# A transformer block in fp32: the gated layer's second projection with seven products in place of eight in three of its four blocks

## Chip, cores and metric

The kernel runs on one core of a Trainium2 chip. The metric is the device time of one execution in microseconds (us). The core has five engines with their own instruction queues: TensorE (PE in the profile; its weight loads are listed apart, as PEld), VectorE (DVE), ScalarE (ACT), GpSimd (POOL) and SyncE (SP), which here issues most of the DMAs. An instruction waits at the head of its engine's queue until the semaphores that it names have been reached.

## Reference

One block on `x` of shape (2, 1024, 256) with a context of shape (2, 154, 192), 16 heads of 64, all in fp32:

```python
h = layernorm(x, ln1_g, ln1_b)
x = attention(h, h, sa_wq, sa_wk, sa_wv, sa_wo, sa_bo) + x
h = layernorm(x, ln2_g, ln2_b)
x = attention(h, cond_emb, ca_wq, ca_wk, ca_wv, ca_wo, ca_bo) + x
h = layernorm(x, ln3_g, ln3_b)
p = h @ ff_w1 + ff_b1                      # 256 -> 2 * 1024
a, gate = p[..., :1024], p[..., 1024:]
h = a * gelu(gate) @ ff_w2 + ff_b2         # 1024 -> 256: the second projection
return h + x
```

The change touches the last product, `(a * gelu(gate)) @ ff_w2`, and what is added to it.

## Kernel before

The kernel has three stages: self-attention, cross-attention and the gated layer. The order of all instructions is written by hand (`tc.manual_schedule()`); the lists `later`, `sums`, `side`, `work` hold small pieces that the main loops take from in a fixed number per step. The framework puts in semaphores for the dependences between engines.

**Tokens and blocks.** The 2048 tokens are 16 tiles of 128 tokens; `xt` keeps all of them on chip. The gated layer works on NPR = 4 blocks (the code calls one a `pair`) of 512 tokens, each with two halves `j` of BT = 256 tokens. The 1024 features are NF = 8 chunks `f` of 128.

**First projection.** The loop `for k in range(2 * FU)` (L1309) has 64 steps. Steps 2n and 2n+1 handle unit n, that is feature chunk f = n % 8 of block n // 8. `gate_first(n)` and `gate_second(n)` issue seven calls of `product` (L1021) for each unit, one of them (number 4, in `gate_last`) a step late; each has 128 x 128 weights and 256 moving columns, and is two matmul instructions in the profile, all of line L1029. DVE adds the partial products in PSUM to the tile `own` (L1052, L1054, L1068, L1071, L1080), ACT copies one (L1048) and evaluates the two gelus (L1066, L1072), and POOL multiplies the two results into `ub[block][j][:, f, :]`, the input of the second projection: L1073 for j = 1 in `gate_second`, L1082 for j = 0 in `gate_last`, which `gate_first` of the next unit calls.

**Second projection.** When chunk 7 of a block is through, `gate_last` puts 32 slots into `sums`: 4 token tiles `i` by 8 chunks. `sum_slot` (L1088) is one call of matmul, 128 tokens by 256 outputs, adding up over the 8 chunks in one PSUM bank; after the eighth, DVE adds the bank to `xt` (L1105) and a DMA stores 128 KB to `out`. The loop takes two slots per step, so block 0 is summed in steps 16 to 31, while block 1 goes through the first projection, and so on. Block 3 has no next block: its 32 slots are issued one after another behind the loop (L1334).

**Other work on POOL in these steps.** `token_sums` (L1006) prepares a block's tokens for the seven products, in steps 8, 24 and 40. `add_biases("ff", b)` leaves in `later` one addition of `ff_b2` per token tile (L324); from step 17 on the loop takes one per step:

```python
if later and (k <= len(CG) + 2 or k > 2 * NF):
    later.pop(0)()
```

**Buffers.** `w2` (`ff_w2`, 8 chunks of 256 outputs) lies with `w1` in one of the two buffers of the tag `pT`; the other held the transposed attention weights of the cross stage and is out of use by step 18. The tile `ends` belongs to the cross stage too. `sum_tile` takes turns between two PSUM banks.

Of the kernel before, what the change touches and what calls it, by code (L numbers as in the profile page):

```python
# [8 lines left out]
F32 = mybir.dt.float32  # L9
AF = mybir.ActivationFunctionType  # L10
ALU = mybir.AluOpType
AX = mybir.AxisListType

P = 128
# [4 lines left out]
def tile_transformer_block(ctx: ExitStack, tc: tile.TileContext, a: dict, out: bass.AP):  # L19
    nc = tc.nc  # L20
    x, cond = a["x"], a["ctx_768"]
    w = {k[len("L0_xattn_"):]: v for k, v in a.items() if k.startswith("L0_xattn_")}
# [9 lines left out]
    NT = S // P  # L32
    GT = 4
# [14 lines left out]
    QH = S // 2  # L48
    GH = QH // QG
    NK = HB // KB  # L50
    TG = HB // T
    NF = DF // P
    SH = GH // 2
    TF = 2
# [8 lines left out]
    pt_ = ctx.enter_context(tc.tile_pool(name="pt", bufs=2))  # L63
# [9 lines left out]
    def sum_tile(name):  # L73

        return ps_o.tile([P, HB], F32, tag="po", name=name)


    xt = {
        (b, g): const.tile([P, GT, D], F32, tag=f"x{b}{g}", name=f"x{b}{g}")
        for b in range(B) for g in range(NG)  # L80
    }
# [10 lines left out]
    names = ["ln1_g", "ln1_b", "ln2_g", "ln2_b", "ln3_g", "ln3_b", "ff_b1"]  # L92
# [5 lines left out]
    for n in names:  # L98
        k = n_of[n]
# [8 lines left out]
    for n in names[:2]:  # L108
        for r0 in range(0, P, HR):
            (nc.scalar if n == names[0] else nc.sync).dma_start(  # L110
                out=cols[r0:r0 + HR, row_of[n]:row_of[n] + NH],
                in_=w[n].rearrange("(r p) -> p r", p=HR),
# [54 lines left out]
    for n in names[2:]:  # L167
        own = rows[row_of[n] - n_cols:row_of[n] - n_cols + n_of[n], :]
        p = HR if n in twice else P
# [42 lines left out]
    ends = const.tile([P, DA // 2], F32, tag="ends", name="ends")  # L212
# [159 lines left out]
    def take_both(dst, pq, mul=None, t0=0, n=S // 2, shared=False):  # L372

        for r in range(2):
            k0, own = r * S // 2 + t0, pq[r][:, :n]
            if mul is not None:
                if shared and r:
                    nc.vector.tensor_scalar(
                        dst[:, k0:k0 + n], own, mul, 1.0, op0=ALU.mult, op1=ALU.mult)
                else:  # L380
                    nc.scalar.activation(dst[:, k0:k0 + n], own, AF.Copy, scale=mul)  # L381
                continue

            dk = dst.rearrange("p (h n j) -> p n h j", h=2, j=KB)[:, k0 // QG:(k0 + n) // QG]
            own = own.rearrange("p (n h j) -> p n h j", h=2, j=KB)
            if shared and r:
                nc.vector.tensor_copy(dk, own)
            else:
                nc.scalar.copy(dk, own)
# [94 lines left out]
    def out_order(kind):  # L484

        return [t for t in tile_order("ff" if kind == "ca" else "ca") if t % 2 == 0]
# [73 lines left out]
    later = []  # L560

    def run(piece):
        done = piece()
        if done is not None:
            (adds if getattr(done, "adds", False) else stores).append(done)

    def flush(queue):
        for fn in queue:
            fn()
        queue.clear()  # L570

    def run_work(n, n_side, bank=None, n_sum=0):

        while n > 0 and work:
            n -= work[0].banks
            run(work.pop(0))
        for _ in range(min(n_side, len(side))):  # L580
            needs_bank, needs, fn = side[0]
            if needs_bank and not bank and n <= 0 or not added.issuperset(needs):
                break
            if needs_bank and not bank:
                n -= 1
            spare["bank"] = bank or mm_tile
            run(fn)
            side.pop(0)
        for i in range(min(max(n, 0) + n_sum, len(outs))):
            spare["out"] = mm_tile if i < n else sum_tile  # L590
            run(outs.pop(0))

    def out_pieces(kind, b, half, tiles):
        outs.extend(lambda t=t: out_piece(kind, b, half, t) for t in tiles)
# [136 lines left out]
    CG = [(t, min(TG, NT - t)) for t in range(0, NT, TG)]  # L731
# [205 lines left out]
    def cross_drain(c):  # L937

        n = c - 2
        if 0 <= n < CA:  # L940
            cross_turn(n)

    def cross_weigh(c):

        ui, n = divmod(c - 2 * len(CG) - 1, len(CG))
        if n == 0 and 0 <= ui < NU:
            for part in range(2):
                run(lambda: cross_values(ui, part))
            flush(stores)


    NPR = B * 2
    BT = S // 4
    FU = NPR * NF
    wsum, wh, ub, psum, pools = {}, {}, {}, {}, {}
# [65 lines left out]
    def product(n, i, into, first):  # L1021

        pair, f = divmod(n, NF)
        own = slice(f * P, (f + 1) * P)
        lhs = {
            1: w1[:, 0, 1, own], 2: w1[:, 1, 1, own], 3: wsum[4][:, own], 4: w1[:, 1, 0, own],
            5: wsum[1][:, own], 6: wsum[2][:, own], 7: w1[:, 0, 0, own],
        }[i]
        nc.tensor.matmul(  # L1029
            into[:, :BT], lhsT=lhs, rhs=wh[pair][i], start=first, stop=True,  # L1030
            skip_group_check=True)
# [24 lines left out]
    def biases(n):  # L1056
        c = row_of["ff_b1"] + n % NF
        return cols[:, c:c + 1], cols[:, c + NF:c + NF + 1]
# [16 lines left out]
    def gate_last(n):  # L1075

        pair, f = divmod(n, NF)
        pa, pb, pc, own = psum.pop(n)
        product(n, 4, pb, False)
        nc.vector.scalar_tensor_tensor(  # L1080
            own[:, 0, :], pb[:, :BT], biases(n)[0], own[:, 0, :], op0=ALU.add, op1=ALU.add)
        nc.gpsimd.tensor_tensor(ub[pair][0][:, f, :], own[:, 0, :], own[:, 3, :], ALU.mult)  # L1082
        if f == NF - 1:
            sums.extend((pair, i, e) for i in range(2 * TF) for e in range(NF))

    sums, summed = [], {}

    def sum_slot():  # L1088

        pair, i, f = sums.pop(0)  # L1090
        if f == 0:
            summed[pair] = sum_tile(f"pf{pair}_{i}")
        own = summed[pair]
        j, e = divmod(i, TF)
        nc.tensor.matmul(  # L1095
            own[:, :D], lhsT=ub[pair][j][:, f, e * P:(e + 1) * P], rhs=w2[:, f, :],
            start=(f == 0), stop=(f == NF - 1),
        )
        if f < NF - 1:
            return None  # L1100
        b, t = divmod(pair * 2 * TF + i, NT)

        def store():
            xs = xt[b, t // GT][:, t % GT, :]
            nc.vector.tensor_tensor(xs, own[:, :D], xs, ALU.add)  # L1105
            (nc.scalar if pair == NPR - 1 and i % 2 else nc.sync).dma_start(
                out=out[b, t * P:(t + 1) * P, :], in_=xs)

        return store


    with tc.manual_schedule():
# [11 lines left out]
        own = [ps_s.tile([P, 2, HB], F32, tag="s", name=f"first_{r}") for r in range(2)]  # L1124
# [7 lines left out]
        def take(what, i):  # L1132
            at = banks[what] if i < 2 else banks["k2"]
            take_both(qk["sa", 0, 0]["qk".index(what)], at, scale if what == "q" else None,
                      i * P, 2 * P, shared=True)
# [36 lines left out]
        for p in range(SA):  # L1172
# [18 lines left out]
            h, hg = divmod(p, SH)  # L1191
            ui, n = divmod(p, 2 * SH)
# [8 lines left out]
            if hg == LAG:  # L1201
                f = (ui - NPAIR // 2 - 1) * EC
# [10 lines left out]
        for c in range(CA):  # L1213
# [7 lines left out]
            if c == SH + 1:  # L1221

                w1, w2, parts = hold_gated()
# [3 lines left out]
            ui, n = divmod(c, len(CG))  # L1227
# [53 lines left out]
            elif n == 2:  # L1281
# [3 lines left out]
                elif ui == HP:  # L1285
                    wo["ca"] = const.tile([P, NPAIR, D], F32, tag="wo", name="ca_wo")
                    later[:0] = [lambda i=i: nc.sync.dma_start(
                        out=wo["ca"][:, i, :], in_=w["ca_wo"][i * P:(i + 1) * P, :])
# [20 lines left out]
        for k in range(2 * FU):  # L1309
            c = CA + k  # L1310
            if k == 0:
                run_work(0, 0, n_sum=2)
            flush(adds)
            (gate_second if k % 2 else gate_first)(k // 2)
            flush(stores)
            flush(lates)
            if k == 2 * len(CG) + 1:
                norm_beside("ff", B - 1)
            cross_drain(c)
            if k % 2:  # L1320
                cross_weigh(c - 1 if k == len(CG) + 2 else c)
            cross_regroup(c)
            if k == len(CG) + 2:
                out_pieces("ca", B - 1, NQ - 1, out_order("ca"))
            if k % (2 * NF) == NF and k < 2 * FU - 2 * NF:
                token_sums(k // (2 * NF) + 1)
            for _ in range(min(2, len(sums))):
                run(sum_slot)
            flush(stores)
            run_work(0 if k == 1 else 1 + k % 2, k % 2)  # L1330
            if later and (k <= len(CG) + 2 or k > 2 * NF):
                later.pop(0)()
        gate_last(FU - 1)
        while sums:  # L1334
            run(sum_slot)
            flush(stores)


# [31 lines left out]
```

## Time and profile before

| | |
|---|---|
| median of 3 runs | 1082.71 us (1082.28 to 1084.15) |
| profiled execution, own time | 1084.96 us |
| its span | 1083.2 us |
| granted TensorE clock | 1.00 |
| PE busy | 1067.0 us, 99% of the span |
| DVE / POOL / ACT busy | 878.7 / 727.1 / 643.5 us (81 / 67 / 59%) |
| second projection, L1095 | 256 matmul instructions of 128 x 256, 63.2 us busy |
| first projection, L1029 | 448 matmul instructions of 128 x 256 |

The span is the time from the first to the last instruction of the profiled execution; 1.8 us of that execution's own time lie outside it. Busy times of PE count a matmul from its start to its modelled end, so that two that follow each other overlap in the records: what one costs is seen from the distance of the starts, called the pitch below.

### The profile page before, as it was taken

Reading aid. Unit: us, or ns where it says so; the run is one execution under the profiler, and the core shown is the slowest. Engines: PE = TensorE matmul, PEld = TensorE weight load, DVE = VectorE, ACT = ScalarE, POOL = GpSimd, SP = SyncE. Lnnn points to the kernel's source line nnn. Section 1 sums busy time; section 2 is a strip of 40 time slices with the busy share of each in tenths; the row PEclk is TensorE's granted clock in tenths of the full one; section 3 lists DMA queues with packets and bytes.
Section 4 is the critical chain, followed back from the end, with each engine's and each line's share of the span. In section 5 each row is a group of like instructions: output and inputs, shape, how many; then the busy total and the mean of one; then the engine's idle time right before and its main releaser. Section 6 shows DMA issues by size and latency. Waiting matters only on the chain.

```text
span 1083.2 us, 46388 instructions
## 1 busy us (share of the span) xinstructions
PE 1067.0 (99%) x19156; PEld 703.2 (65%) x19156; DVE 878.7 (81%) x1297; ACT 643.5 (59%) x2062; POOL 727.1 (67%) x1552
## 2 busy tenths in 40 slices
PE   8999999999999999999999999999999999999998
PEld 6556556556565565575665655566776677788887
DVE  5799999998989989999999889968877887654442
ACT  5766666777667657666776776656555554242321
POOL 2677777777777777677777777776756785475321
PEclk9999999999999999999999999999999999999999
DMA  3222122112111121111111101136765545000000
GB/s 91 68 70 52 39 48 53 43 43 50 32 43 34 30 50 38 34 43 34 33 42 25 43 14 38 29 79 150 191 157 125 119 107 118 1 10 15 11 14 30
DMA packets 104724, 60.81 MB, mean 56 GB/s; under 512 B 32378, under 2 KB 95298, under 8 KB 104514
## 3 DMA queue, kind: packets, MB, share of 16 engines
q1 hardware_dynamic: 103138, 57.07, 22.2%
q8 instruction: 151, 2.47, 1.0%
q10 hardware_dynamic: 1376, 0.79, 0.2%
q14 instruction: 59, 0.48, 0.1%
HBM read 27.91 MB, written 2.10 MB: 28 GB/s over the span
## 4 chain that ended last, share of the span: by engine, by line
PE 83%; DVE 4%; POOL 4%; DMA 3%; SPq 2%; ACT 2%; issue 1%; POOLq 0%; DVEq 0%; ACTq 0%
PE po L549 18%; PE s L497 17%; PE py_sa L471 5%; PE pf L1095 5%; PE py_ca L471 5%; PE pk_sa L366 4%; PE pv_sa L397 4%; PE poc L908 4%; PE pq_ca L366 4%; PE pq_sa L366 4%; PE pb L1029 4%; DMA st<-st 3%; PE sc L828 2%; PE pa L1029 2%; PE pc L1029 2%; SPq L518 2%
## 5 line engine op out<-in xcount | busy, mean ns | idle before, releaser
L619 POOL TENSOR_SCALAR p<-p,rd,ee 128x512 f32<-128x512 f32 x512 | 390.4, 768 | 90.8 <-DVE rd L609 87.7
L508 ACT ACTIVATE p<-s,st 128x512 f32<-128x512 f32 x512 | 345.0, 686 | 171.1 <-DVE st L681 163.7
L681 DVE TENSOR_REDUCE st<-s 128x2 f32<-128x1024 f32 x256 | 308.5, 1206 | 56.9 <-issue 19.0
L644 DVE STREAM_TRANSPOSE pT<-p 128x1024 f32<-128x1024 f32 x256 | 302.7, 1219 | 2.4 <-POOL p L619 2.1
L497 PE MATMUL s<-k_sa,q_sa 64*32 64x512 f32 x4096 | 252.8, 591 | 3.3 <-ACT p L508 2.5
L549 PE MATMUL po<-pT,v_sa 64*32 64x256 f32 x8192 | 237.1, 376 | 1.0 <-DVE pT L644 1.0
L549 PEld LDWEIGHTS po<-pT,v_sa 64*32 64x32 f32 x8192 | 172.9, 106 | 76.2 <-issue 31.2
L497 PEld LDWEIGHTS s<-k_sa,q_sa 64*32 64x32 f32 x4096 | 78.4, 106 | 104.6 <-issue 57.6
L845 ACT ACTIVATE p<-sc,neg 128x154 f32<-128x154 f32 x256 | 96.1, 403 | 83.0 <-DVE rden L853 79.3
L856 POOL TENSOR_SCALAR p<-p,rden 128x154 f32<-128x154 f32 x256 | 96.8, 398 | 56.7 <-DVE rden L853 56.5
L508 ACT ACTIVATION_READ_ACCUMULATOR p<-s,st 128x1 f32 x512 | 103.9, 203 | 0.0
L526 POOL TENSOR_TENSOR dd<-st 128x8 f32<-128x8 f32 x128 | 25.6, 200 | 74.9 <-DMA st<-st 73.0
L397 PEld LDWEIGHTS pv_sa<-sa_wv,hT_ln 64*128 64x128 f32 x1024 | 58.5, 188 | 14.2 <-issue 8.4
L397 PE MATMUL pv_sa<-sa_wv,hT_ln 64*128 64x128 f32 x1024 | 61.8, 275 | 0.0
L471 PE MATMUL py_ca<-ca_wo,o_ca 128*128 128x256 f32 x256 | 60.0, 382 | 0.5 <-DVE o_ca L922 0.5
L366 PE MATMUL pq_ca<-hT_ln,ca_wq 64*64 64x512 f32 (+1 forms) x544 | 60.1, 590 | 0.0
L471 PE MATMUL py_sa<-sa_wo,o_sa 128*128 128x256 f32 x256 | 59.7, 385 | 0.2 <-ACT v_sa L406 0.2
L471 PEld LDWEIGHTS py_sa<-sa_wo,o_sa 128*128 128x128 f32 x256 | 47.3, 190 | 18.2 <-issue 6.9
L834 DVE TENSOR_REDUCE neg<-sc 128x6 f32<-128x924 f32 (+1 forms) x48 | 47.9, 998 | 13.7 <-PE sc L828 13.3
L366 PE MATMUL pq_sa<-hT_ln,sa_wq 64*32 64x512 f32 (+1 forms) x976 | 56.6, 586 | 0.0
L366 PE MATMUL pk_sa<-hT_ln,sa_wk 64*32 64x512 f32 x960 | 56.2, 590 | 0.3 <-ACT q_sa L381 0.3
L845 ACT ACTIVATION_READ_ACCUMULATOR p<-sc,neg 128x1 f32 x256 | 56.1, 219 | 0.0
(121 smaller groups left out, 1418.9 us busy)
## 6 DMA issues: line engine op xcount, KB each, us to landing
wf<-pT_ca SPq DMA_DIRECT2D x128, 128.0 KB
st<-st SPq DMA_DIRECT2D x512, 1.0 KB
v_sa<-v_sa SPq DMA_DIRECT2D x32, 256.0 KB
sa_wq<-in_L_xattn_sa_wq_dram SPq DMA_DIRECT2D x32, 128.0 KB
sa_wk<-in_L_xattn_sa_wk_dram SPq DMA_DIRECT2D x32, 128.0 KB
sa_wv<-in_L_xattn_sa_wv_dram SPq DMA_DIRECT2D x32, 128.0 KB
ca_wq<-in_L_xattn_ca_wq_dram SPq DMA_DIRECT2D x32, 128.0 KB
wf<-in_L_xattn_ff_w_dram SPq DMA_DIRECT2D x12, 256.0 KB
```

Of the source, the lines that this page charges most:

```text
L366: nc.tensor.matmul(pq[r][f:f + m, at:at + n], lhsT=wt[own, c, f:f + m], rhs=h[own, c, t0:t0 + n], start=(c == 0), stop=(c == NH - 1), tile ...
L397: nc.tensor.matmul(pv[r][:, i * P:(i + 1) * P], lhsT=h[own, c, i * P:(i + 1) * P], rhs=wt[own, c, :], start=(c == 0), stop=(c == NH - 1), ...
L471: nc.tensor.matmul(py[:, e * D:(e + 1) * D], lhsT=o[:, i, (t + e) * P:(t + e + 1) * P], rhs=wo[kind][:, g * HP + i, :], start=(i == 0), st ...
L497: nc.tensor.matmul(sc[a4 * KB:(a4 + 1) * KB, j, :], lhsT=q[r, c:c + KB], rhs=k[r, h * HB:(h + 1) * HB], start=True, stop=True, tile_positi ...
L508: nc.scalar.activation(pr[:, j, :], sc[:, j, :], AF.Exp, bias=st[:, 0, 0, i, j:j + 1], accum_out=st[:, 0, 1, i, j:j + 1],)
L549: nc.tensor.matmul(po[a2][d:d + KB, :QH // 2], lhsT=v[r, t, e, d:d + KB], rhs=pT[r, d // DH * NK + n, :], start=(t == 0 and e == 0), stop= ...
L619: nc.gpsimd.tensor_scalar(pr[:, j, :], pr[:, j, :], own["rd"][:, c:c + 1], own["ee"][:, 0, c:c + 1], op0=ALU.mult, op1=ALU.mult,)
L644: nc.vector.transpose(halves[h][:, :, c:c + KB], slots[p]["p"][i].rearrange("p j (n k) -> p (j n) k", k=KB))
L681: nc.vector.tensor_reduce(st[:, 0, 0, i, :], sc[i], AX.X, ALU.max, negate=True)
L845: nc.scalar.activation(pr_[:, j, i, :T], sc[:, j, i * T:(i + 1) * T], AF.Exp, bias=neg[:, j, i:i + 1], accum_out=den[:, j, i:i + 1],)
L856: nc.gpsimd.tensor_scalar(pr_[:, j, i, :T], pr_[:, j, i, :T], rden[:, j, i:i + 1], 1.0, op0=ALU.mult, op1=ALU.mult,)
L1029: nc.tensor.matmul(into[:, :BT], lhsT=lhs, rhs=wh[pair][i], start=first, stop=True, skip_group_check=True)
```

## The change

In blocks 1, 2 and 3 (`FAST`) the second projection is no longer 8 chunks added up. The features are split into even and odd chunks, the 256 tokens of a half into two tiles, and the outputs into two halves of 128, so that the product is one of 2 x 2 blocks; seven block products take the place of eight, with sums of the inputs beforehand and sums of the results behind.

- `hold_quick` takes a new tile in the free `pT` buffer for the sums, and two pieces of `ends` for copies.
- `quick_weights` makes four combinations of `w2`, each 128 x 512 elements, on POOL (put in at step 18).
- `quick_tokens` makes four combinations per half and even/odd couple of chunks, each 128 x 128, on POOL; one of them overwrites a quarter of `ub`. The list `combos` holds them; each step takes two. For the last unit, half 1 has its four on DVE.
- `fast_sum` is one of the seven products: four calls of matmul (eight instructions) of 128 tokens by 128 outputs. Products 0 and 1 share a PSUM bank, so do 2 to 4, and 5 and 6, the later added onto the earlier; between two of them the partial sum is read. Behind product 0 ACT copies the bank and POOL (DVE in the last block) adds the copy to three quarters of the two token tiles; behind each other product DVE adds the bank to one quarter. A step takes one `fast_sum`; a block has 14 (two halves by seven). The two stores of a half follow products 5 and 6.
- In the last block the two halves take turns, product by product, with more PSUM banks.
- From step 17 on, a bias addition is taken only in odd steps.

```diff
--- before.py
+++ after.py
@@ -1080,14 +1080,117 @@
         nc.vector.scalar_tensor_tensor(
             own[:, 0, :], pb[:, :BT], biases(n)[0], own[:, 0, :], op0=ALU.add, op1=ALU.add)
         nc.gpsimd.tensor_tensor(ub[pair][0][:, f, :], own[:, 0, :], own[:, 3, :], ALU.mult)
-        if f == NF - 1:
-            sums.extend((pair, i, e) for i in range(2 * TF) for e in range(NF))
-
-    sums, summed = [], {}
-
-    def sum_slot():
-
-        pair, i, f = sums.pop(0)
+        if pair in FAST and f % 2:
+            for j in (1, 0) if pair == NPR - 1 else (0, 1):
+                engine = nc.vector if n == FU - 1 and j else nc.gpsimd
+                combos.extend(((pair, j), fn) for fn in quick_tokens(pair, j, f // 2, engine))
+        if f == NF - 1 and pair in FAST:
+            order = [(j, g) for j in range(2) for g in range(7)]
+            if pair == NPR - 1:
+                order = [(j, g) for g in range(7) for j in (1, 0)]
+            sums.extend((lambda j=j, g=g: fast_sum(pair, j, g), 2) for j, g in order)
+        elif f == NF - 1:
+            sums.extend(
+                (lambda i=i, e=e: sum_slot(pair, i, e), 1) for i in range(2 * TF) for e in range(NF))
+
+    sums, summed, quick, combos, mixed = [], {}, {}, [], {}
+    FAST = range(1, NPR)
+    NHF = NF // 2
+
+    def hold_quick():
+
+        own = pt_.tile([P, 2 * NK, QH // 2], F32, tag="pT", name="quick").rearrange("p a b -> p (a b)")
+        at = 0
+
+        def take(*dims):
+            nonlocal at
+            n = 1
+            for d in dims:
+                n *= d
+            view = own[:, at:at + n]
+            at += n
+            names = "abc"[:len(dims)]
+            return view.rearrange(
+                f"p ({' '.join(names)}) -> p {' '.join(names)}", **dict(zip(names, dims)))
+
+        for i in (1, 2, 3, 4):
+            quick["w", i] = take(NHF, P)
+        for i in range(4):
+            quick["u", i] = take(3, NHF, P)
+        for i in range(2):
+            quick["own", i] = ends[:, i * P:(i + 1) * P]
+
+    def quick_weights():
+
+        (b11, b12), (b21, b22) = (
+            [w2[:, h::2, d * P:(d + 1) * P] for d in range(2)] for h in range(2))
+        t1, t2, t3, t4 = (quick["w", i] for i in (1, 2, 3, 4))
+        tt = nc.gpsimd.tensor_tensor
+        return [
+            lambda: tt(t1, b12, b11, ALU.subtract),
+            lambda: tt(t2, b22, t1, ALU.subtract),
+            lambda: tt(t3, b22, b12, ALU.subtract),
+            lambda: tt(t4, b21, t2, ALU.subtract),
+        ]
+
+    def quick_tokens(pair, j, c, engine=nc.gpsimd):
+
+        u, own = ub[pair][j], quick["u", (2 * pair + j) % 4]
+        (a11, a12), (a21, a22) = (
+            [u[:, 2 * c + h, e * P:(e + 1) * P] for h in range(2)] for e in range(2))
+        s1, s2, s4 = (own[:, i, c, :] for i in range(3))
+        tt = engine.tensor_tensor
+        mixed[pair, j] = mixed.get((pair, j), 0) + 1
+        return [
+            lambda: tt(s1, a21, a22, ALU.add),
+            lambda: tt(s2, s1, a11, ALU.subtract),
+            lambda: tt(a21, a11, a21, ALU.subtract),
+            lambda: tt(s4, a12, s2, ALU.subtract),
+        ]
+
+    def fast_sum(pair, j, g):
+
+        u, own = ub[pair][j], quick["u", (2 * pair + j) % 4]
+        (a11, a12), (a21, a22) = (
+            [u[:, h::2, e * P:(e + 1) * P] for h in range(2)] for e in range(2))
+        assert g < 2 or mixed[pair, j] == NHF and (pair, j) not in [key for key, _ in combos]
+        lhs = (a11, a12, own[:, 1], a21, a22, own[:, 0], own[:, 2])[g]
+        rhs = (
+            w2[:, ::2, :P], w2[:, 1::2, :P], quick["w", 2], quick["w", 3], quick["w", 4],
+            quick["w", 1], w2[:, 1::2, P:])[g]
+        if g in (0, 2, 5):
+            bank = sum_tile
+            if pair == NPR - 1:
+                bank = {0: sum_tile, 2: mm_tile, 5: part_tile}[g]
+            summed[j] = bank(f"pq{pair}_{j}_{g}")
+        into = summed[j][:, :P]
+        for c in range(NHF):
+            nc.tensor.matmul(
+                into, lhsT=lhs[:, c, :], rhs=rhs[:, c, :], start=(g in (0, 2, 5) and c == 0),
+                stop=(c == NHF - 1), skip_group_check=True)
+        b, t = divmod(pair * 2 * TF + 2 * j, NT)
+        xs = xt[b, t // GT][:, t % GT:t % GT + 2, :].rearrange("p t (h d) -> p (t h) d", d=P)
+
+        def store():
+            if g == 0:
+                nc.scalar.copy(quick["own", j], into)
+                (nc.vector if pair == NPR - 1 else nc.gpsimd).tensor_tensor(
+                    xs[:, 1:, :], xs[:, 1:, :],
+                    quick["own", j].unsqueeze(1).to_broadcast([P, 3, P]), ALU.add)
+                return
+            q = (None, 0, 1, 3, 2, 3, 1)[g]
+            nc.vector.tensor_tensor(xs[:, q, :], into, xs[:, q, :], ALU.add)
+            if g > 4:
+                e = 6 - g
+                queue = nc.scalar if pair == NPR - 1 and e else nc.sync
+                queue.dma_start(
+                    out=out[b, (t + e) * P:(t + e + 1) * P, :],
+                    in_=xt[b, (t + e) // GT][:, (t + e) % GT, :])
+
+        return store
+
+    def sum_slot(pair, i, f):
+
         if f == 0:
             summed[pair] = sum_tile(f"pf{pair}_{i}")
         own = summed[pair]
@@ -1324,15 +1427,26 @@
                 out_pieces("ca", B - 1, NQ - 1, out_order("ca"))
             if k % (2 * NF) == NF and k < 2 * FU - 2 * NF:
                 token_sums(k // (2 * NF) + 1)
-            for _ in range(min(2, len(sums))):
-                run(sum_slot)
+            n_left = 2
+            while n_left > 0 and sums:
+                fn, n = sums.pop(0)
+                n_left -= n
+                run(fn)
             flush(stores)
+            if k == 2 * NF + 2:
+                hold_quick()
+                combos[:0] = [(None, fn) for fn in quick_weights()]
+            for _ in range(min(2, len(combos))):
+                combos.pop(0)[1]()
             run_work(0 if k == 1 else 1 + k % 2, k % 2)
             if later and (k <= len(CG) + 2 or k > 2 * NF):
-                later.pop(0)()
+                if k <= len(CG) + 2 or k % 2:
+                    later.pop(0)()
         gate_last(FU - 1)
+        while combos:
+            combos.pop(0)[1]()
         while sums:
-            run(sum_slot)
+            run(sums.pop(0)[0])
             flush(stores)
```

## Prediction

> **What bounds the kernel now.** I read the page first, then a table of windows over the last 128 us, where the edited code runs, then the waits there, and last the timeline around single instructions.
>
> ```profile
> span 1083.2 us, 46388 instructions
> PE 1067.0 (99%) x19156; PEld 703.2 (65%) x19156; DVE 878.7 (81%) x1297; ACT 643.5 (59%) x2062; POOL 727.1 (67%) x1552
> PEclk9999999999999999999999999999999999999999
> ```
>
> TensorE (PE) is busy from end to end at the full clock. The windows are cut at the steps in which block 0, 1 and 2 are summed (16 to 31, 32 to 47, 48 to 63), and the tail with block 3:
>
> ```profile
> core 0: us, PE busy (x) PEld busy (x) DVE busy (x) ACT busy (x) POOL busy (x), PEclk, DMA share, GB/s
> 955.00:991.00 36.00, 36.00 (x173) 31.69 (x172) 17.20 (x42) 12.20 (x27) 24.47 (x36) 1.00 0.04 12
> 991.00:1028.00 37.00, 37.00 (x173) 32.58 (x172) 18.16 (x44) 10.46 (x23) 14.01 (x21) 1.00 0.04 15
> 1028.00:1066.00 38.00, 38.00 (x178) 33.45 (x177) 18.74 (x45) 10.83 (x24) 11.63 (x17) 1.00 0.05 15
> 1066.00:1083.20 17.20, 13.85 (x65) 11.85 (x63) 2.25 (x6) 0.00 (x0) 1.28 (x2) 1.00 0.11 38
> ```
>
> PE has no idle time until the tail ends; VectorE (DVE) is half free; GpSimd (POOL) is two thirds full in the first window and a third in the next two. The waits between 960 and 1081 us say the same: POOL, ACT and DVE wait for PE or for each other, and no row names PE as the one that waits. So here the time is what PE issues. The rows that carry the summing:
>
> ```profile
> DVE x L1105 <- PE pf L1095: 17.5, 16, 3.0
> 1065.88 13.98 PE L1095 MATMUL pf<-wf,u 128*128 128x256 f32 x64
> 1079.89 0.42 DVE L1105 TENSOR_TENSOR x<-pf,x 128x256 f32<-128x256 f32 x1 [3.03 <-PE pf L1095]
> ```
>
> The tail's 64 instructions start (13.98 - 0.38) / 63 = 0.2158 us apart (0.38 is the modelled length of the last). That is the pitch of every 128x256 matmul in the stage.
>
> **Part 1: the products.** Removed for each of three blocks: 32 calls, 64 instructions of 256 columns, 64 x 0.2158 = 13.81 us. Added: 14 products of 8 instructions with 128 columns, 112 in all. Seven for eight saves only if half the columns take half the time, although each instruction still loads 128x128 weights, with a recorded length of 190 ns. The trace has 128-column matmuls on the whole array, the transposes, and an fp32 projection directly behind them:
>
> ```profile
> 960.54 0.60 PE L284 MATMUL ph_ln<-ident,xn_ln 128*128 128x128 f32 x4
> 960.98 0.60 PE L1029 MATMUL pa<-hT_ln,wf 128*128 128x256 f32 x2
> 960.87 0.19 PEld L1029 LDWEIGHTS pa<-hT_ln,wf 128*128 128x128 f32 x1
> ...
> 9.40 1.16 PE L366 MATMUL first<-hT_ln,sa_wq 64*128 64x128 f32 x16
> ```
>
> Four 128-column instructions and then the projection: (960.98 - 960.54) / 4 = 0.11, more exactly (0.60 - 0.273) / 3 = 0.109 us apart, 0.273 being the median length of one. The last of these four gaps holds the very load in question: the projection's 190 ns load starts at 960.87, with the last transpose, and its matmul 0.11 us later. So the end of a load's record lies beside the start of its own matmul. 112 x 0.1093 = 12.24 us, a gain of 1.57 us a block, 4.71 us in three. The less kind row: the first stage's query projection, sixteen 64x128 instructions in pairs (last line), takes (1.16 - 0.272) / 15 = 0.059 for one, 0.118 for a pair; 112 x 0.118 = 13.22, a gain of 0.59 a block, 1.8 in all. I take 0.1093, from the same tile shape and stage, and keep 1.8 for the range.
>
> A rule speaks against this. The Trainium skill, page "TensorE: Matmul & The Clock Gate", section "The mechanism" of the part on packing small matmuls, says that a weight load runs beside matmuls in flight only when the row groups differ, and here all instructions use all rows. Taken at its word, the record's 190 ns would stand ahead of each 109 ns matmul, 112 x 0.299 = 33.5 us, or 59 us slower in three blocks, an estimate by that page. The rows above show a load inside the preceding matmul of the same rows, so the row decides.
>
> **Part 2: reading a bank between two products.** Within a group of a half (0-1, 2-3-4, 5-6) the next product adds to a bank that must be read first: four waits a half. What PE waits for: the last instruction's record ends 0.16 us after PE is free for the next (0.273 - 0.109); 0.04 until DVE starts; the addition, 128 columns, is 0.30 us by the line through 256 columns (425 ns) and 512 (653); about 0.05 back. That is 0.55 us; the ACT copy of product 0 is shorter (L777, 128x128: 259 ns). One product a step leaves six instructions (`gate_second`, 1.30 us) or eight (`gate_first`, 1.73 us) between them, and DVE's own additions of that step are through by then (in the trace the last ends 0.25 us before the old slots do). In the tail the other half's product, 0.87 us, lies between. Cost nothing; without that cover, 16 waits in blocks 1 and 2 would cost up to 8.8 us.
>
> One lull has no cover. Steps 46, 47, 62 and 63 have no product left to issue. After 63, `gate_last` issues product 4 onto the bank that DVE reads after product 7, with only product 3 between: 0.38 + 0.04 + 0.48 (L1080's form) + 0.05 = 0.95 after the last start of product 7, against 0.65 of issue. **+0.30 us**. After 47, product 1 of the next unit fills it.
>
> **Part 3: POOL.** No trace row has a 128x128 addition on POOL. By rows of the same operation, 128x8 takes 200 ns (L526) and 128x256 727:
>
> ```profile
> 966.79 0.73 POOL L324 TENSOR_TENSOR x<-x,ff_b 128x256 f32<-128x256 f32 x1
> 967.48 0.73 POOL L1082 TENSOR_TENSOR u<-own 128x256 f32<-128x256 f32 x1
> 972.92 0.72 POOL L1012 TENSOR_TENSOR hs<-hT_ln 128x256 f32<-128x256 f32 x1
> 973.72 0.73 POOL L1013 TENSOR_TENSOR hs<-hT_ln,hs 128x256 f32<-128x256 f32 x1
> 974.40 0.73 POOL L1014 TENSOR_TENSOR hT_ln<-hT_ln 128x256 f32<-128x256 f32 x1
> ```
>
> Starts are 0.69 apart, 0.80 where an operation reads the result of the one before (L1013). So 128 columns are 455 ns, 0.415 in pitch, 0.53 behind a direct producer; one of the four combinations is such: 0.445 on average. Bounds: 0.20 (128x8) and 0.69 (128x256).
>
> Steps 18 to 31, POOL: `quick_weights` 4 x 1.27 = 5.1 (512 columns on the same line), products 14 x 0.69 = 9.7, `token_sums` 2.9, seven bias additions 4.8 (fourteen before), 24 combinations 10.7: 33.2 us. PE in the same steps: 98 + 56 instructions at 0.2158, 33.2 us. Steps 32 to 47: products 11.0, `token_sums` 2.9, bias 5.5, two additions of 384 columns 2.0, 32 combinations 14.2: 35.6 us against PE's 112 x 0.2158 + 12.24 = 36.4. So POOL becomes full, but not over. It may lag: a product first needs what POOL wrote a step earlier (product 1 needs chunk 7, product 2 the second combination), about 2.5 us of room. I put 0.2 us for waits; at 0.53 throughout, the lag grows by 2.0 + 2.0, of which some 1.5 us shows.
>
> What is queued behind on POOL: the unit's own multiplications, whose readers come a block later, and `token_sums`, used eight steps later. Seven buffers of `own` allow a lag of some three units. No DMA waits for POOL but through the additions to `xt`, and those come before DVE's in the same half, two steps apart.
>
> **Part 4: the rest.** DVE: 12 additions of 0.30 a block for 4 of 0.425, +1.9 us in 37 with half of them free. ACT: two copies a block. The stores are the same in number and size (four of 128 KB a block, on SP's queue, in the tail half on ACT's); behind the last addition the tail is the same, and that addition is 0.12 shorter. Sum: -4.71 + 0.30 + 0.2 - 0.1 = **-4.3 us**. The profiled run took 1084.96, so it would take 1080.6; set against the median of 1082.71, **1078.4 us**. About 0.2%, 2.2 us, is what a measurement of this kernel can tell from no change.
>
> **Rivals.**
> 1. *POOL late in part* (chance 0.13): combinations at a pitch of 0.5 to 0.58, because more of them read each other, or because the 128-column pitch is the query projection's: gain 0.5 to 3, about 1080.7. For it: the tally above leaves under 1 us free. Half of this is within 0.2%.
> 2. *POOL becomes the bound, slower* (0.10): place, the products 1 and 2 of blocks 1 and 2, which wait for POOL. At the upper bound of 0.69 the stretches hold 39.0 and 43.5 us for PE's 33.2 and 36.4, 12.9 over, less 2.5 of room: 10 us of waits, 1088.4. It decides from the pitch at which waits eat 4.5 us: 24 (x - 0.445) + 32 (x - 0.47) = 7, x = 0.58. Against it: 200 ns for 128x8 shows that the fixed part is small.
> 3. *The load shows* (0.07): 13.81 / 112 = 0.123 us is the pitch at which nothing is gained; at the recorded 190 ns a block takes 21.3 us, 22.4 us slower in all, 1105. Against it: the load at 960.87.
> 4. *The products do what they say but the bank reads or DVE's order give it back* (0.06): about no change, 1082.5.
>
> **Chances.** My forecast 0.64, with an own range of 1077 to 1080. Faster by over 0.2%: 0.64 + 0.07 + 0.01 (from the fourth) = 0.72. Within: 0.06 + 0.05 = 0.11. Slower: 0.17. The range runs from 1077.2 (no POOL wait, and the 0.7 that runs differ by below the median) to 1082.8, past rivals 1 and 4; it leaves out 2 and 3 and a little below.
>
> **What would show it.** Right: 128x128 matmuls of `pq` about 0.109 us apart with no PE wait between; the tail's 112 instructions in some 12.4 us; POOL's 128x128 rows near 455 ns; POOL busy over 90% between steps 18 and 47. Wrong: PE rows that wait for POOL's `u` or `quick`, for DVE's additions to `xt`, or a pitch above 0.12.

## The result, and the profile after

The changed kernel takes 1079.73 us (median, 1079.12 to 1080.74) against 1084.11 us for the kernel before in the same rounds: a ratio of 0.9966, 95% interval 0.9955 to 0.9977. At the before median of 1084.11 this is 3.7 us less, by the interval 2.5 to 4.9. The two medians lie 4.4 us apart, the means of the same five runs 3.7 us (1083.54 and 1079.79). Later rounds of the same two kernels gave 0.9963 (0.9951 to 0.9976).

The page's first lines and, below them, the windows of the profile after, cut at nearly the same steps as before (the first row stands for steps 18 to 31, not 16 to 31; columns: busy time and number of instructions by engine, granted clock, DMA share, GB/s):

```profile
span 1078.0 us, 46825 instructions
...
PE 1062.9 (99%) x19300; PEld 697.1 (65%) x19300; DVE 887.4 (82%) x1327; ACT 645.6 (60%) x2068; POOL 774.9 (72%) x1652
...
PEclk9999999999999999999999999999999999999999
```

```profile
953.00:986.00 33.00, 33.00 (x159) 29.05 (x158) 16.03 (x39) 10.87 (x24) 31.24 (x51) 1.00 0.04 13
986.00:1022.50 36.50, 36.50 (x225) 33.64 (x224) 19.68 (x50) 11.01 (x26) 32.36 (x58) 1.00 0.05 16
1022.50:1062.00 39.50, 39.35 (x237) 35.61 (x236) 22.61 (x57) 11.94 (x28) 30.93 (x59) 1.00 0.05 17
1062.00:1078.00 16.00, 12.91 (x114) 12.67 (x113) 7.09 (x20) 1.04 (x3) 4.72 (x8) 0.99 0.10 34
```

PE is still busy from end to end. POOL, which was two thirds and then a third busy, is now 95% busy in the first row and 89% in the second. That is the price of the sums, and in this kernel it costs no time.

How near it is to costing some can be read where block 2's product 1 loads the last chunk that POOL writes (start, length, engine, line, operation, count):

```profile
1028.39 0.73 POOL L1082 TENSOR_TENSOR u<-own 128x256 f32<-128x256 f32 x1
1029.19 0.19 PEld L1168 LDWEIGHTS pq<-wf,u 128*128 128x128 f32 x1
```

The load starts 0.07 us behind the end of L1082; a load that has to wait for L1082 starts 0.05 us behind it (e2 and e4 below). So 0.02 us of room is left in block 2, and none in the profile of the later rounds; in block 1 the load comes 1.17 us behind, which leaves 1.12 us. It is used below as the **room**.

The spans differ by 5.2 us, more than the times do, because 1.4 us of it lies ahead of the edited code: the first matmul of the second projection starts at 952.33 us before and at 950.90 after, and in later profiled runs of other kernels with the same code up to there it starts anywhere from 950.4 to 954.2. So kernels are compared below by the **stage**, from the start of the first matmul of the second projection to the start of the last. It is 127.14 us before and 123.73 after, and 123.73 again in the profile of those later rounds: **-3.41 us**. What follows the last start fell from 3.70 to 3.41 us. Together -3.70, as in the ratio.

Where these come from, in single instructions. The last first-projection pair ahead of the tail, the products in the tail and the last addition, from the timeline:

```profile
1061.71 0.70 PE L1029 MATMUL pb<-hs,wf 128*128 128x256 f32 x2
...
1067.60 3.74 PE L1168 MATMUL pq<-quick,u 128*128 128x128 f32 x32
...
1074.95 0.29 DVE L1182 TENSOR_TENSOR x<-pq,x 128x128 f32<-128x128 f32 x1 [0.60 <-PE pq L1168]
```

(3.74 - 0.275) / 31 = 0.1118 us apart, 0.275 being the mean length of one; over all of them the starts are 0.1116 apart. The L1029 pair takes 0.70 where two matmuls take 0.59: it is the wait ahead of the tail, 0.52 us from the start before the pair to its first start and 0.32 between its two, where 0.216 is the pitch. The only waits of PE and its weight loads that a program row names between step 18 and the end:

```profile
PEld pb L1029 <- DVE own L1068: 0.5, 1, 0.5
```

And POOL's combinations (busy time, mean ns):

```profile
L1147 POOL TENSOR_TENSOR u<-u 128x128 f32<-128x128 f32 x23 | 10.8, 470 | 0.0
L1146 POOL TENSOR_TENSOR quick<-quick,u 128x128 f32<-128x128 f32 x23 | 10.7, 465 | 1.8
L1145 POOL TENSOR_TENSOR quick<-u 128x128 f32<-128x128 f32 x23 | 10.6, 461 | 0.4
L1148 POOL TENSOR_TENSOR quick<-u,quick 128x128 f32<-128x128 f32 x23 | 10.5, 458 | 0.0
L1177 POOL TENSOR_TENSOR x<-x,ends 128x384 f32<-128x384 f32 x4 | 4.0, 997 | 0.0
```

### The profile page after: what moved, and what is told of

Its sections match the earlier page's. It is cut to its first block, busy times and chain, and to the rows that moved or that the text cites. A ratio compares the mean times of both kernels' runs of the same rounds, so it can differ in the third digit from the quotient of the medians.

```text
span 1078.0 us, 46825 instructions
## 1 busy us (share of the span) xinstructions
PE 1062.9 (99%) x19300; PEld 697.1 (65%) x19300; DVE 887.4 (82%) x1327; ACT 645.6 (60%) x2068; POOL 774.9 (72%) x1652
## 4 chain that ended last, share of the span: by engine, by line
PE 87%; POOL 3%; DMA 3%; DVE 3%; SPq 2%; issue 1%; ACT 1%; POOLq 0%; DVEq 0%; ACTq 0%
PE s L497 19%; PE po L549 19%; PE py_sa L471 5%; PE py_ca L471 5%; PE pv_sa L397 5%; PE pk_sa L366 4%; PE pq_sa L366 4%; PE pq_ca L366 4%; PE poc L908 4%; PE pb L1029 4%; PE pq L1168 3%; PE sc L828 3%; PE pa L1029 2%; PE pc L1029 2%; SPq L518 2%; DMA st<-st 2%
## 5 line engine op out<-in xcount | busy, mean ns | idle before, releaser
L549 PEld LDWEIGHTS po<-pT,v_sa 64*32 64x32 f32 x8192 | 168.9, 106 | 79.5 <-issue 32.3
```

What stands on the lines that cost most here:

```text
L549: nc.tensor.matmul(po[a2][d:d + KB, :QH // 2], lhsT=v[r, t, e, d:d + KB], rhs=pT[r, d // DH * NK + n, :], start=(t == 0 and e == 0), stop= ...
```

## Experiments

The theory: in these steps the time is what PE issues, 0.2158 us for a 256-column and 0.1116 us for a 128-column instruction, plus waits that can be named; POOL just fits. Rivals: the gain comes from elsewhere (the bias additions, the variation ahead of the stage); POOL has room to spare; the 128-column pitch is set by the columns and not by the load.

| kernel | stage, us | against before |
|---|---|---|
| before | 127.14 | |
| changed | 123.73 | -3.41 |
| e1 block 1 only | 125.83 | -1.31 |
| e2 bias additions in each step | 126.67 | -0.47 |
| e3 bias spread alone | 127.14 | 0.00 |
| e4 one more addition on POOL per step | 131.86 | +4.72 |
| e5 block 1 with 64 columns | 136.24 | +9.10 |
| e6 last steps covered | 123.32 | -3.82 |
| e7 half of the sums on DVE | 124.47 | -2.67 |
| e8 e6 and half of block 0 | 123.34 | -3.80 |

**One block alone.**

```diff
-    FAST = range(1, NPR)
+    FAST = range(1, 2)
```

> Seven products in block 1 alone; blocks 2 and 3 are summed as before. Measured by the stage: start of the first second-projection matmul to start of the last one, 127.14 us before and 123.74 after in the profiled runs. Theory (PE's issue alone sets the time): one block saves 64 x 0.2158 - 112 x 0.1116 = 1.31 us, and with old slots in steps 62 and 63 there is no wait ahead of the tail: stage 125.8 us. Rival (part of the gain comes from the bias additions moved apart or from another place): stage clearly below 125.5 us. Rival (fixed costs of the sums eat a block's gain): 126.5 or more.

Stage 125.83 us: one block is worth 1.31 us, as 64 x 0.2158 - 112 x 0.1116 says, and no gap stands ahead of the tail. Three such blocks are -3.93; with the +0.41 us of the gaps that is -3.52, and the changed kernel has -3.41. The remaining 0.10 us is how the stage is measured: it ends with the start of the last instruction, so that block 3, which comes last, is counted without its last pitch, 0.2158 before and 0.1116 after. This 0.10 us is found in what follows the last start.

**The bias additions.** First the change without their spreading, then the spreading without the change.

```diff
-                if k <= len(CG) + 2 or k % 2:
-                    later.pop(0)()
+                later.pop(0)()
```

> The changed kernel, but with a bias addition taken in every step from 17 on, as before the change. Theory (POOL just fits in steps 18 to 31; lag up to one step is hidden): seven more additions of 0.69 us, 4.8 us, before block 1 is summed; less 2.2 to 2.5 us of room, PE waits about 2.5 us for POOL at product 1 of block 1, and the stage is 126.2 us, so most of the gain is lost. Rival (POOL has room enough, spreading the additions does nothing): stage 123.7 us and no PE row that waits for POOL.

Stage 126.67 us, ratio to the kernel before 0.9992 (0.998 to 1.0005): no change that can be told from none. The waits of PE and of its loads:

```profile
PE pq L1168 <- POOL u L1082: 2.4, 2, 2.0
```

```profile
PEld pq L1168 <- POOL u L1082: 2.8, 2, 2.2
```

The rows are of products 0 and 1 of block 1, which wait for POOL's chunks 6 and 7 (L1082); only the second was expected, and the changed kernel has neither. The longer wait in the timeline:

```profile
994.13 0.72 POOL L1082 TENSOR_TENSOR u<-own 128x256 f32<-128x256 f32 x1
994.91 0.19 PEld L1168 LDWEIGHTS pq<-wf,u 128*128 128x128 f32 x1 [2.23 <-POOL u L1082]
```

In the starts, the two gaps are 0.64 and 2.32 us in place of 0.11, 2.7 us in sum; behind each of them the next start is 0.10 late too (0.213 us for 0.112), and the stage is 2.94 longer. POOL's account gives the same: counted from the first matmul of the second projection, chunk 7 of block 1 is ready at 44.50 us instead of 40.44, and 4.06 less the 1.12 us of room is 2.94. So seven additions of 0.69 us on an engine that PE does not wait for in the changed kernel decide over most of the gain.

```diff
             if later and (k <= len(CG) + 2 or k > 2 * NF):
-                later.pop(0)()
+                if k <= len(CG) + 2 or k % 2:
+                    later.pop(0)()
```

> The kernel before, with the bias additions taken in odd steps only. Theory (PE's issue sets the time, and POOL is a third to two thirds full there): nothing, stage 127.1 us. Rival (the spreading itself is part of the gain): stage 126.5 us or less.

Stage 127.14 us, the same to the hundredth. The spreading brings nothing itself; it makes the room that the sums need.

**POOL's limit.**

```diff
+            if combos and k >= 2 * NF + 4:
+                nc.gpsimd.tensor_tensor(
+                    ends[:, 3 * P:], w2[:, 0, :P], w2[:, 1, :P], ALU.add)
             for _ in range(min(2, len(combos))):
```

> The changed kernel with one more 128x128 addition on POOL, onto a scratch piece, in each step that makes combinations (20 to 63). Theory (POOL nearly full): 12 x 0.41 = 5.0 us more in steps 20 to 31 and 6.6 us in 32 to 47; less the room, PE waits 2.5 to 3 us in block 1 and 4.5 to 5 us in block 2 at products 1, so +7.5 to 8 us: stage 131.5 us. Rival (POOL's idle time, 9 us between 953 and 1022 us, takes it): stage below 126 us.

Stage 131.86 us, +8.1 against the changed kernel; all of the gain and 4.7 us more are gone. The waits of PE, and the window of the longest of them with the two behind it:

```profile
PE pq L1168 <- POOL u L1082: 5.2, 3, 2.2
```

```profile
994.00:996.00 2.00, 0.56 (x4) 0.53 (x5) 0.03 (x1) 0.00 (x0) 2.00 (x4) 1.00 0.00 0
996.00:998.00 2.00, 2.00 (x7) 1.61 (x6) 0.75 (x2) 0.37 (x1) 1.92 (x5) 0.55 0.00 0
998.00:1000.00 2.00, 2.00 (x11) 1.82 (x10) 0.85 (x2) 0.00 (x0) 2.00 (x5) 0.60 0.01 4
```

The size fits, its parts less so. PE waits at products 0 and 1 of both blocks, for chunks 6 and 7. In block 1 the gaps are 0.31 and 2.35 us over the pitch, as expected, but in block 2 only 1.65 and 1.67 in place of 4.5 to 5; behind each of the four the next start is 0.10 late. The clock gives the rest: after the gap of 2.46 us the granted clock (the number behind POOL's in a row) is 0.55 and 0.60 in two windows; six 256-column matmuls start 0.43 us apart instead of 0.216 and four of 128 columns 0.21 instead of 0.112, 1.7 us that no wait shows. Together 6.0 + 0.4 + 1.7 = 8.1 us.

POOL's account shows why the parts could shift. Chunk 7 of block 2 is ready 86.31 us after the first matmul of the second projection instead of 78.22; 8.09 less the 0.02 us of room is all but 0.06 of the loss. PE waits for POOL on both sides of the slow stretch, and POOL is idle for only 1.2 us between chunk 7 of block 1 and chunk 7 of block 2 (3.6 in the changed kernel). So the time that the slow clock took is time that PE would else have waited in block 2; that was not tried alone. The rival's 9 us of idle time do not stand in the profile: POOL has 5.8 us of it between 953 and 1022 us in the changed kernel.

**What sets the pitch of a 128-column matmul.** The changed kernel, in block 1 each call split into two of 64 columns with the same weights (the sums of this kernel are not those of the reference; the question needs only the number, the sizes and the order of the instructions). The loop over the two halves `d` stands where the three points are:

```diff
-                into, lhsT=lhs[:, c, :], rhs=rhs[:, c, :], start=(g in (0, 2, 5) and c == 0),
...
+                into[:, own_d], lhsT=lhs[:, c, :], rhs=rhs[:, c, own_d],
+                start=(g in (0, 2, 5) and c == 0),
```

> Block 1's products are issued with 64 columns instead of 128, so 224 instructions with the same 128x128 weights for 112. If the weight load sets the pitch of 0.1116: 224 x 0.1116 = 25.0 us, +12.5, stage 136.2 us, pitch 0.11. If the columns set it: pitch 0.056 to 0.06, stage 123.7 to 124.7. If a load adds a part of its time to each: between, pitch 0.06 to 0.11.

Stage 136.24 us, +12.51 for 112 more instructions: 0.1117 us each. The timeline of one product, and its loads in the groups:

```profile
992.59 1.89 PE L1170 MATMUL pq<-wf,u 128*128 128x64 f32 x16
```

```profile
L1170 PEld LDWEIGHTS pq<-wf,u 128*128 128x128 f32 x128 | 15.7, 192 | 0.5
```

Half the columns save nothing: the loads still start 0.112 us apart. It is not a least time of the matmul either: the first two matmuls of each product start 0.056 us apart, and the first stage's sixteen pairs of a 64x128 load and a matmul (in the prediction) 0.059. So a row of 128x128 fp32 loads goes on at 0.1116 us a load, and a matmul of fewer columns gains nothing; with 256 columns the load is covered. 128 columns lie just under this edge: half of 0.2158 is 0.108, and the first gap of a product in the changed kernel's steps is 0.109.

**The two gaps ahead of the tail.**

```diff
-            n_left = 2
+            n_left = 0 if k in (2 * FU - 11, 2 * FU - 7) else 2
```

> The changed kernel; steps 53 and 57 take no product of block 2, so that its last two fall in steps 62 and 63. Theory: the two gaps ahead of the tail (0.52 and 0.32 us against 0.216) are gone, -0.41, stage 123.3 us. Rival (the gap moves to steps 53 and 57, or product 1 of block 2 comes late): 123.7 us.

Stage 123.32 us, -0.41, no gap anywhere, no wait of PE in the profile. One time of 1080.70 us; a gain of 0.04% is too small for the rounds to show.

**Half of the sums on DVE.**

```diff
-                engine = nc.vector if n == FU - 1 and j else nc.gpsimd
+                engine = nc.vector if j else nc.gpsimd
```

> The changed kernel, but the combinations of half 1 are on DVE in all three blocks, not for the last unit alone. Theory: POOL has 7 us less in a block and DVE some 16 x 0.3 to 0.8 us more; neither is the bound, stage 123.7 us within 0.2; beside POOL a DVE addition with both inputs in SBUF takes longer than the 0.29 us of one that reads PSUM, as the four in the tail of the changed kernel do (0.28 to 0.81), and POOL's grow from 0.455 too. Rival (DVE held up behind POOL's products): PE waits for DVE's reads of the banks, stage 125 us or more.

Stage 124.47 us, 0.74 longer, between the two expectations: at the idle steps 46 and 47, 62 and 63, DVE reads the bank late (gaps of 0.69 and 0.32, and of 0.32, 0.53 and 0.32 us against 0.216; the last two stand in the changed kernel too). The same addition on the two engines:

```profile
L1147 DVE TENSOR_TENSOR u<-u 128x128 f32<-128x128 f32 x12 | 7.5, 629 | 0.0
L1147 POOL TENSOR_TENSOR u<-u 128x128 f32<-128x128 f32 x12 | 6.0, 496 | 0.0
L1182 DVE TENSOR_TENSOR x<-pq,x 128x128 f32<-128x128 f32 x36 | 10.3, 290 | 15.2 <-PE pq L1168 15.2
```

The run holds its own comparison: of DVE's 48 additions of the combinations (L1145 to L1148), 16 fall where POOL is idle and take 0.28 to 0.29 us; the other 32, beside an instruction of POOL, take 0.28 to 0.82 us, 0.61 on average.

**A further half block.** On top of e6, half 1 of block 0 by seven products too, its sums on DVE in steps 18 to 25.

```diff
+            sums.extend((lambda g=g: fast_sum(pair, 1, g), 2) for g in range(7))
...
-            n_left = 2
+            n_left = 0 if k in (2 * FU - 11, 2 * FU - 7) else 2
...
+                early.extend(fn for c in range(NHF) for fn in quick_tokens(0, 1, c, nc.vector))
+            for _ in range(min(2, len(early))):
+                early.pop(0)()
```

> The changed kernel with the last steps covered (steps 53 and 57 free) and with seven products in half 1 of block 0 as well, its sixteen combinations on DVE in steps 18 to 25 so that POOL gets no more. Theory: against the changed kernel -0.41 for the gaps and -1.31 / 2 = -0.65 for the half block, stage 122.7 us, about 4.8 us under the kernel before. Rival (DVE additions with both inputs in SBUF slow POOL, which has no room in steps 18 to 31): PE waits 0.5 us or more for POOL at product 1 of block 1 or for DVE at the banks, stage 123.2 us or more.

> The changed kernel as it is, on the chip and in the rounds of the run before this, for comparison: stage 123.7 us, 3.7 us under the kernel before by the sum of stage and tail, a ratio of 0.9966.

Stage 123.34 us: of the 1.06 us expected under the changed kernel, 0.39 came. The rival's place and size hold: one gap of 0.68 us at product 1 of block 1, where PE waits for POOL, and the next start 0.10 late, 0.67 us in all.

```profile
PE pq L1169 <- POOL u L1082: 0.4, 1, 0.4
...
L1082 POOL TENSOR_TENSOR u<-own 128x256 f32<-128x256 f32 x6 | 4.5, 748 | 0.0
L1147 DVE TENSOR_TENSOR quick<-quick,kT 128x128 f32<-128x128 f32 x4 | 3.1, 767 | 0.1
...
976.98 1.00 POOL L1178 TENSOR_TENSOR x<-x,ends 128x384 f32<-128x384 f32 x1
```

POOL is late for two reasons, and the rival names one of them. Beside DVE's sums its operations take longer: L1082 takes 748 ns between 950 and 975 us, where it takes 726 in the changed kernel, and the operations that both kernels have, in the same order, are 0.85 us behind by 977 us. And POOL has an operation more, which the expectation overlooked: behind product 0 of the new half it adds the copy to 384 columns (L1178, the last line). Chunk 7 of block 1 is ready 1.14 us later than in the changed kernel, PE comes to it 0.65 us earlier, and with 1.12 us of room that makes the 0.67 us. How much each of the two reasons would cost alone was not tried.

The ratio to the kernel before is 0.9972 (0.9962 to 0.9981), the changed kernel's in the same rounds 0.9963 (0.9951 to 0.9976): no better. The profiles agree: what follows the last start is 3.90 us here and 3.42 in the changed kernel of these rounds, because the last store lands 0.44 us later after it, so that stage and end together are 127.24 and 127.15 us. Why it lands later was not found; e4 has 3.72 us there, the other changed kernels that end with the same code 3.41 or 3.42.

## Why the prediction was right, point by point

- **The mechanism** (PE issue bounds, everything else must stay hidden): shown by e1, e3 and e6, each within 0.05 us of what the count of instructions says (for e6, 127.14 - 3.93 + 0.10 = 123.31 against 123.32), and by e2, e4 and e8, which lose the time by which POOL comes too late.
- **The products**, -4.71 predicted, -3.93 measured. The mis-sized term is the pitch: I took 0.1093 from the transposes, whose loads are recorded at 140 ns, although the fp32 load's record of 190 ns stood beside it. The one gap that held such a load is 0.109 in the trace too, but that is a single one behind the short loads of the transposes. In the changed kernel's steps the first gap of a product is 0.109 as well, and only behind it, load upon load, 0.1116: one load told nothing of a row of them. With e5: it is the load, 0.1116, and not the columns. My less kind bound, 0.118, was too slow.
- **The rule of the Trainium skill** (page "TensorE: Matmul & The Clock Gate", section "The mechanism", a load beside a matmul only in other row groups): taken at this word no run here agrees with it; the load's record of 0.19 us starts 2 ns behind the start of a matmul of the same rows. The section also lets a load into the background weight buffer be pulled ahead, and no run here shows whether these are such loads. The same page, section "LDWEIGHTS (loading the stationary operand)", gives the number of columns divided by 1.2 as a load's nanoseconds, by which 128 columns are an estimated 107 ns; the runs show 0.1116 us between loads, in fp32.
- **The gap ahead of the tail**, +0.30 predicted, +0.41 measured: the chain through L1068 gives 0.31, and the matmul behind it starts 0.10 late as well, which I had not counted.
- **POOL**, 0.2 us of waits predicted, none measured. The durations by the line through two sizes were right: 455 ns predicted, 458 to 470 measured; 384 columns, 997 measured as on the line; a pitch of 0.53 behind a producer and 0.41 else, 0.443 on average against 0.445. "Full, but not over" held, in block 2 by luck: of the 2.5 us of room, 1.12 are left in block 1 and 0.02 in block 2, where the tally had 35.6 us of work for 36.4. So that no wait at all is seen there is a matter of hundredths. The prediction looked at product 1 alone; with more work on POOL product 0 waits too (e2, e4).
- **The reads of the banks** were covered, as worked out: no PE row waits for L1176 or L1182.
- **The tail's end**, -0.1 predicted, -0.29 measured: the shorter addition (425 to 291 ns) and the shorter matmul record (379 to 275), which I had left out. Of this, 0.10 is the last pitch of block 3, which the -3.93 holds already: -3.93 + 0.41 - 0.19 = -3.71.
- **Rivals**: 1 and 2 did not come true, but a little more work on POOL brings them (e2, e4); 3 did in its direction, at a fraction of its size (0.1116, not 0.19 or 0.123); 4 did not.

The sum was -4.3 and the measurement -3.7: the pitch is 0.78 too good, the other terms together 0.2 too bad, so that the errors cancel in part. Set against the median of three runs that gave 1078.4 us, and 1079.73 was measured.

## What to carry to other kernels

A saving in products that shortens the instructions comes in full only while the columns of one instruction take longer than its weight load; here 128 fp32 columns lie just under that size, and 7 for 8 with half the columns gives 9.5% of the projection's issue in place of 12.5%. Count the engine that takes over the sums by stretch, not by its share of the span: POOL's 72% hid a stretch of 95%, and a bias addition more in every second step would have cost most of the gain. Better still, look up how long each result is ready before its reader: a result's lateness less that room gave the losses of e2, e4 and e8 to 0.06 us. Where an operation of the right size is missing from a trace, a line through two sizes of the same operation, and the pitch instead of the length, were good to about 3%.

## What was unexpected of the hardware

- An addition of 128x128 on DVE with both inputs in SBUF takes 0.28 to 0.29 us where POOL is idle, as one that reads PSUM does (0.29), and up to 0.82 us beside POOL (e7); the means of POOL's four additions grow from 458 to 470 ns to 467 to 496. The Trainium skill, page "GPSIMD Engine Reference", section "Specifications", says that POOL shares its SBUF interfaces with VectorE and that DVE instructions with two SBUF inputs contend; the runs agree.
- After one gap of 2.46 us between two starts of PE (e4) the granted clock stood at 0.55 and 0.60 in the next two windows of 2 us, and for 3.4 us PE's starts were twice as far apart; after gaps of 1.8 us (e4) and 2.32 us (e2) they were not. Where the limit lies, and what it goes by, these runs do not show.
